# Two-layer graph attention on one core: a new order of the opening loads and projections, two-head folding of a weight, the last sums on TensorE, squares from the evicted copy, and all additions on GpSimd

## The chip, the cores and the metric

One core of a Trainium2 chip runs the whole program. The metric is device time in microseconds (us) of that core; a kernel's figure is the median of its runs. A profile is one further look at one execution; its span is some 2 us shorter than the time of that run.

In this kernel tiles lie in one memory, SBUF, and TensorE writes its products to another, PSUM, in banks; an "eviction" is an instruction of another engine that copies a product out of PSUM. In profile lines PE is TensorE, PEld its weight loads, DVE VectorE, ACT ScalarE and POOL GpSimd. A line of a chain (the work that ended last, followed back) has start and duration in us, engine, tile and line of the kernel; a line of a timeline has the operation and shape too, and in brackets how long the engine sat idle before it and who released it. `x16` merges 16 entries; one product in fp32 shows as two entries. A line of a stretch has its length, then busy time and entries of PE, PEld, DVE, ACT and POOL, the granted clock, and two figures for the DMA.

"Period" is the stretch in which the kernel does one step of its software pipeline; there are 65 of them, and the steady ones are the "middle".

## The reference, cut to what matters

There are 64 graphs of 256 tokens with 512 features. Each passes through two layers of attention over its adjacency.

```python
h = relu(layernorm(x))
# layer 0, 8 heads of 64
m = h @ map_w.T + map_b
n = m / max(norm(m per head), 1e-8);  cos = n @ n.T
p = softmax(mask(q(m) @ k(m).T / 8)) * keep
adj = (cos > 0.1) * p
Ax = adj @ (h @ gcn_map_w.T + gcn_map_b)
out = relu(Ax @ gcn_W.T / (adj.sum(-1) + 1))
x = x + out
# layer 1, 4 heads of 64
x = x + softmax(mask(q1 @ k1.T / 8)) @ v1 @ Wo + bo,  from relu(layernorm(x))
```

`gcn_W` is folded into `gcn_map_w` once at the start, into a weight `wc`, and its bias into `bc`.

## The kernel before

A period works on three graphs: `g` in layer 0, `b` (the one before) in layer 1, and `nx` and `n2` (the next ones) in their projections. TensorE's products go to PSUM through a ring of eight banks. Every call of `bank` takes the next one; it is free when whoever reads it has done so.

```python
def mapped(g):                       # m of a graph, features first
    for n in range(NKC // 2):
        p = features_first(w.wm, g.hT, (2 * n, 2 * n + 1), ...)
        sq = sb2.tile([P, 2, S], F32, tag="sq", ...)
        for k in range(2):
            m = 2 * n + k
            nc.scalar.activation(sq[:, k, :], p[:, k, :], AF.Square, bias=w.bm[:, m:m + 1])
            nc.vector.tensor_scalar_add(g.mT[:, m, :], p[:, k, :], w.bm[:, m:m + 1])

def far_off(g, c, co, eng):          # keeps e where cos > 0.1, and prepares the sums
    g.q[c] = far(co, g.e[c], ...)    # VectorE: a = (co > 0.1) * e, two instructions
    eng.tensor_add(g.e[c], g.e[c], g.q[c])
    g.d[c] = halves(eng, g.e[c], ...)

def period(i):
    ...
    if g:
        spread(g)                                             # p_b
        g.e = [exps(products(g.kT, g.qT, c, ...), ...) for c in range(NKC)]
    if nx:
        mapped(nx)                                            # p_m
    for c in range(NKC):
        if g: co[c] = products(g.nT, g.nT, c, ...)            # co
        if b and c == 1: sc = [products(b.k1T, b.q1T, k, ...) for k in range(NIC)]
        if g and c < 2: far_off(g, c, co[c], nc.gpsimd)
    ...                              # e1 of b, far_off 2 (GpSimd) and 3 (VectorE), d1 of b (VectorE)
    ...                              # messages, queries of nx
    if b:
        values1(b); sums1(b); divided(b)                      # av, zb, then z, rz, oT
    if g:
        values(g, 0); values(g, 1); sums(g)                   # av, sm
    if nx: p_n = norms(nx)
    if b: result(b, 0)                                        # p_o, needs oT
    ...
```

In the opening the weights are loaded and folded first, with temporary tiles; when their pool closes, the tiles of the loop take over its memory. Graphs 0 and 1 are then made ready together.

Of the kernel before, what the change touches and what calls it, by code (L numbers as in the profile page):

```python
# [28 lines left out]
class Weights:  # L29


    def __init__(self, nc, const, tmp, psum, a):
        P, D, DH = 128, a["x"].shape[2], 64
        H0, NKC = D // DH, D // P
        self.ident = const.tile([P, P], F32, name="ident")
        make_identity(nc, self.ident)
        self.ident_b = const.tile([P, P], BF16, name="ident_b")
        nc.vector.tensor_copy(self.ident_b, self.ident)
        self.ones = const.tile([P, DH], F32, name="ones")
        nc.vector.memset(self.ones, 1.0)  # L40
        self.blk = const.tile([P, P], F32, name="blk")
        nc.vector.memset(self.blk, 0.0)
        for j in range(P // DH):
            nc.vector.memset(self.blk[j * DH:(j + 1) * DH, j * DH:(j + 1) * DH], 1.0)



        self.blk32 = const.tile([P, 32], F32, name="blk32")
        nc.vector.memset(self.blk32, 0.0)
        self.sel = const.tile([P, 2, P], F32, name="sel")  # L50
        for j in range(2):
            nc.vector.memset(self.blk32[j * DH:(j + 1) * DH, j * 16:(j + 1) * 16], 1.0)
            for k in range(2):
                r = 32 * k + 16 * j
                nc.vector.tensor_add(self.sel[:, k, j * DH:(j + 1) * DH], self.ident[:, r:r + 1].to_broadcast([P, DH]),
                                     self.ident[:, r + DH:r + DH + 1].to_broadcast([P, DH]))

        def load_w(ap, name):
            t = const.tile([P, ap.shape[0] // P, ap.shape[1]], F32, name=name)
            nc.gpsimd.dma_start(out=t, in_=ap.rearrange("(c p) f -> p c f", p=P))  # L60
            return t

        def load_b(ap, name):
            t = const.tile([P, D // P], F32, name=name)
            nc.gpsimd.dma_start(out=t, in_=ap.rearrange("(c p) -> p c", p=P))
            return t

        self.wm, self.bm = load_w(a["map_wT"], "wm"), load_b(a["map_b"], "bm")
        self.wc = const.tile([P, NKC, D], F32, name="wc")
        self.bc = const.tile([P, D], F32, name="bc")  # L70

        gt = const.tile([DH, DH], F32, name="gt")
        nc.gpsimd.dma_start(out=gt, in_=a["gcn_WT"])
        gb = const.tile([DH, H0], F32, name="gb")
        nc.gpsimd.dma_start(out=gb, in_=a["gcn_map_b"].rearrange("(h j) -> j h", j=DH))
        gbb = tmp.tile([DH, H0, P], F32, name="gbb")
        nc.vector.tensor_copy(gbb, gb[:, :, None].to_broadcast([DH, H0, P]))
        p_bc = psum.tile([P, D], F32, tag="w", name="p_bc")
        for h in range(H0):
            nc.tensor.matmul(p_bc[:, h * DH:(h + 1) * DH], gbb[:, h, :], gt, start=True, stop=True)  # L80
        nc.vector.tensor_copy(self.bc, p_bc)
        gw = tmp.tile([DH, H0, D], F32, name="gw")
        nc.gpsimd.dma_start(out=gw, in_=a["gcn_map_w"].rearrange("(h j) f -> j h f", j=DH))
        for c in range(NKC):
            p_wc = psum.tile([P, D], F32, tag="w", name=f"p_wc{c}")
            for h in range(H0):
                nc.tensor.matmul(p_wc[:, h * DH:(h + 1) * DH], gw[:, h, c * P:(c + 1) * P], gt,
                                 start=True, stop=True)
            nc.vector.tensor_copy(self.wc[:, c, :], p_wc)
        self.wq, self.bq = load_w(a["q_wT"], "wq"), load_b(a["q_b"], "bq")  # L90
        self.wk, self.bk = load_w(a["k_wT"], "wk"), load_b(a["k_b"], "bk")
        self.wq1, self.wk1 = load_w(a["Wq"], "wq1"), load_w(a["Wk"], "wk1")
        self.wv1, self.wo1 = load_w(a["Wv"], "wv1"), load_w(a["Wo"], "wo1")
        self.bo_b = const.tile([P, D], F32, name="bo_b")
        bo = a["bo"]
        nc.gpsimd.dma_start(out=self.bo_b, in_=bass.AP(tensor=bo.tensor, offset=bo.offset, ap=[[0, P], [1, D]]))
# [3 lines left out]
def fast_path(ctx, tc, a, w, chk, out):  # L100
# [30 lines left out]
    def load(i):  # L131
        g = Graph()
        g.i, g.q, g.d = i, {}, {}
# [67 lines left out]
    def mapped(g):  # L201
        g.mT = sb1.tile([P, NKC, S], F32, tag="mT", name=f"mT{g.i}")
        g.sq = []
        for n in range(NKC // 2):
            p = features_first(w.wm, g.hT, (2 * n, 2 * n + 1), f"p_m{g.i}_{n}")
            sq = sb2.tile([P, 2, S], F32, tag="sq", name=f"sq{g.i}_{n}")
            for k in range(2):
                m = 2 * n + k
                nc.scalar.activation(sq[:, k, :], p[:, k, :], AF.Square, bias=w.bm[:, m:m + 1])  # L209
                nc.vector.tensor_scalar_add(g.mT[:, m, :], p[:, k, :], w.bm[:, m:m + 1])  # L210
            g.sq.append(sq)
# [74 lines left out]
    def halves(eng, e, name):  # L286
        d = sb2.tile([P, 2, S], F32, tag="d", name=f"d{name}", bufs=6)
        eng.tensor_add(d, e[:, :, :S], e[:, :, S:])  # L288
# [9 lines left out]
    def far_off(g, c, co, eng):  # L298

        g.q[c] = far(co, g.e[c], f"{g.i}_{c}")  # L300
        eng.tensor_add(g.e[c], g.e[c], g.q[c])  # L301
        g.d[c] = halves(eng, g.e[c], f"0_{g.i}_{c}")
# [7 lines left out]
    def sums(g):  # L310
        sm = bank(f"sm{g.i}")
        for n in range(2):
            for k in range(4):
                nc.tensor.matmul(sm[32 * k:32 * (k + 1), n, :], w.ones[:, :32], g.d[2 * n + k // 2][:, k % 2, :],
                                 start=True, stop=True)
# [33 lines left out]
    def sums1(b):  # L349
        zb = bank(f"zb{b.i}")  # L350
        for c in range(NIC):
            for s in range(2):
                nc.tensor.matmul(zb[s * DH:(s + 1) * DH, c, :], w.ones, b.d1[c][:, s, :], start=True, stop=True)  # L353
# [3 lines left out]
    def divided(b):  # L357
        rz = sb1.tile([P, NIC, S], F32, tag="rz", name=f"rz{b.i}")
# [3 lines left out]
        nc.scalar.activation(b.z, rz, AF.Copy, accum_out=chk[:, b.i, 3:4])  # L362
# [7 lines left out]
    def period(i):  # L370
# [10 lines left out]
        for c in range(NKC):  # L381
# [4 lines left out]
            if g and c < 2:  # L386
                far_off(g, c, co[c], nc.gpsimd)
        if b:
            b.e1 = [exps(sc[k], b.mask1, f"1_{b.i}_{k}") for k in range(NIC)]
        if g:  # L390
            far_off(g, 2, co[2], nc.gpsimd)
            far_off(g, 3, co[3], nc.vector)
        if b:
            b.d1 = [halves(nc.vector, b.e1[k], f"1_{b.i}_{k}") for k in range(NIC)]
# [20 lines left out]
        if nx:  # L415
            p_n = norms(nx)
        if b:
# [45 lines left out]
    with tc.manual_schedule():  # L463
        graphs = {n: load(n) for n in range(min(3, B))}
        for n in range(min(2, B)):
# [5 lines left out]
            graphs[n].hT = turned(graphs[n], f"0_{n}")  # L471
        g = graphs[0]
        mapped(g)
        p_n = norms(g)
# [3 lines left out]
        messages(g, 0)  # L478
        messages(g, 1)
        for n in range(2):  # L480
            queries(g, n)
            keys(g, n)
        for i in range(B + 1):
# [205 lines left out]
def two_layer_kernel(  # L689
# [25 lines left out]
    with tc.tile_pool(name="wtmp", bufs=1) as tmp, \  # L715
            tc.tile_pool(name="wps", bufs=2, space=bass.MemoryType.PSUM) as psum:
        w = Weights(nc, const, tmp, psum, a)
# [48 lines left out]
```

## Time and profile before

| | before |
|---|---|
| time, median of 3 runs | 4140.31 us (4139.12 to 4140.85) |
| span of the profile | 4136.5 us |
| start of period 0 (p_b, the spread of the norms) | 71.13 us |
| one period in the middle | 63.30 us |
| TensorE busy | 4076.0 us |

The lines that bound the kernel are in the prediction. First the chain in one period (start, us, what), then VectorE's timeline, then four entries of the last co products on TensorE, taken with a window of 0.16 us:

```profile
2101.53 1.93 PE co L267 x16
2103.45 1.73 PE sc L267 x16
2105.18 1.98 PE co L267 x15
2107.15 7.06 PE p_s L218 x16
```

```profile
2102.07 0.48 DVE L210 TENSOR_SCALAR mT<-p_m,bm 128x256 f32<-128x256 f32 x1 [1.70 <-ACT sq L209]
2103.10 0.48 DVE L210 TENSOR_SCALAR mT<-p_m,bm 128x256 f32<-128x256 f32 x1 [0.54 <-ACT sq L209]
2103.50 2.47 DVE L282 SCALAR_TENSOR_TENSOR a<-co,e 128x512 f32<-128x512 f32 x4
```

### The profile page before, as it was taken

What the parts mean: (1) busy time and instruction counts of PE and PEld (TensorE: products, weight loads), DVE (VectorE), ACT (ScalarE), POOL (GpSimd) and SP (SyncE); (2) the same over time, 40 slices, a digit from 0 to 9 for tenths busy, and PEclk for the clock granted to TensorE, in tenths of its full rate; (3) what the DMA queues carried; (4) which work ended last, traced back from release to release, by engine and by line L of the source; (5) the groups of instructions that cost most, each with busy time, mean ns of one, the idle gap of its engine ahead of it and who ended that gap; (6) DMA issues with size and microseconds to landing.
All of it is one profiled execution on the core that took longest, in us unless ns stands there. A gap on an engine that the chain in (4) does not pass through costs nothing.

```text
span 4136.5 us, 56746 instructions
## 1 busy us (share of the span) xinstructions
PE 4076.0 (99%) x23633; PEld 3099.0 (75%) x23633; DVE 2649.1 (64%) x3415; ACT 1480.4 (36%) x3138; POOL 1332.9 (32%) x788
## 2 busy tenths in 40 slices
PE   8999999999999999999999999999999999999997
PEld 6777777777777777777777777777777777777774
DVE  3576576676665766766766657667667566576674
ACT  2433433333333333333333333333333433333332
POOL 2233233232332432333323324323333233233232
PEclk9999999999999999999999999999999999999998
DMA  2000000000000000000000000000000000000000
GB/s 87 12 17 17 23 12 22 22 12 23 22 12 23 13 21 22 12 23 22 12 23 20 14 23 12 22 23 12 22 22 12 23 17 17 23 12 22 22 6 16
DMA packets 54389, 81.57 MB, mean 20 GB/s; under 512 B 19744, under 2 KB 19760, under 8 KB 54128
## 3 DMA queue, kind: packets, MB, share of 16 engines
q1 hardware_dynamic: 52224, 71.32, 5.2%
q0 software_dynamic: 1904, 6.58, 0.5%
q8 instruction: 188, 3.08, 0.3%
q14 instruction: 73, 0.60, 0.0%
HBM read 44.33 MB, written 33.55 MB: 19 GB/s over the span
## 4 chain that ended last, share of the span: by engine, by line
PE 91%; DVE 6%; ACT 2%; issue 0%; DMA 0%; POOL 0%; ACTq 0%; POOLq 0%; DVEq 0%
PE p_k L177 16%; PE p_q L177 16%; PE p_m L177 11%; PE p_s L218 11%; PE sc L267 8%; PE co L267 6%; PE p_o L367 6%; PE p_v L452 5%; DVE rz L359 5%; PE av L295 3%; PE p_t L167 3%; PE p_b L238 2%; PE zb L353 1%; PE p_l L336 1%; ACT z L362 1%; ACT z L355 1%
## 5 line engine op out<-in xcount | busy, mean ns | idle before, releaser
L301 POOL TENSOR_TENSOR e<-e,a 128x1024 f32<-128x1024 f32 x192 | 576.5, 3003 | 1719.9 <-DVE a L282 1719.9
L275 DVE TENSOR_TENSOR e<-e,mask 128x1024 f32<-128x1024 f32 x384 | 593.1, 1599 | 142.6 <-ACT e L274 142.6
L242 DVE TENSOR_TENSOR nT<-mT,p_b 128x512 f32<-128x512 f32 x128 | 82.2, 683 | 727.1 <-PE p_b L238 727.1
L177 PE MATMUL p_m<-hT,wm 128*128 128x256 f32 x2048 | 459.8, 383 | 0.0
L218 PE MATMUL p_s<-wc,hT 128*128 128x512 f32 x1024 | 456.6, 599 | 0.0
L177 PE MATMUL p_k<-mT,wk 128*128 128x256 f32 x2048 | 452.8, 379 | 0.0
L177 PE MATMUL p_q<-mT,wq 128*128 128x256 f32 x2048 | 452.6, 379 | 0.0
L177 PEld LDWEIGHTS p_q<-mT,wq 128*128 128x128 f32 x2048 | 389.1, 190 | 80.2 <-issue 30.6
L177 PEld LDWEIGHTS p_m<-hT,wm 128*128 128x128 f32 x2048 | 384.5, 190 | 70.7 <-ACT e L274 20.9
L250 ACT ACTIVATE qT<-p_q,bq 128x256 f32<-128x256 f32 x256 | 107.5, 471 | 889.9 <-PE p_q L177 889.9
L177 PEld LDWEIGHTS p_k<-mT,wk 128*128 128x128 f32 x2048 | 384.2, 190 | 49.6
L274 ACT ACTIVATE e<-sc 128x512 f32<-128x512 f32 x768 | 389.7, 618 | 80.3 <-PE sc L267 79.6
L340 POOL TENSOR_TENSOR xs<-xs,o 128x512 f32<-128x512 f32 x128 | 159.9, 1271 | 783.9 <-DVE o L338 783.9
L218 PEld LDWEIGHTS p_s<-wc,hT 128*128 128x128 f32 x1024 | 189.3, 190 | 235.6 <-issue 235.3
L288 DVE TENSOR_TENSOR d<-e 128x512 f32<-128x512 f32 x192 | 344.3, 1844 | 2.2
L288 POOL TENSOR_TENSOR d<-e 128x512 f32<-128x512 f32 x192 | 318.5, 1659 | 15.1
L282 DVE SCALAR_TENSOR_TENSOR a<-co,e 128x512 f32<-128x512 f32 x512 | 316.2, 677 | 0.0
L267 PE MATMUL co<-nT 64*128 64x256 f32 x2048 | 266.3, 387 | 1.2 <-DVE a L282 1.2
L367 PE MATMUL p_o<-wo,oT 128*128 128x512 f32 x512 | 248.9, 609 | 15.6 <-ACT z L362 10.5
L359 DVE RECIPROCAL rz<-z 128x512 f32<-128x512 f32 x64 | 214.6, 3354 | 71.5 <-ACT z L355 71.5
L210 DVE TENSOR_SCALAR mT<-p_m,bm 128x256 f32<-128x256 f32 x256 | 123.2, 481 | 186.5 <-ACT sq L209 186.5
L439 POOL TENSOR_TENSOR xs<-xs,bo_b 128x512 f32<-128x512 f32 x128 | 171.0, 1356 | 221.5 <-DVE xn L158 217.8
(113 smaller groups left out, 5920.6 us busy)
## 6 DMA issues: line engine op xcount, KB each, us to landing
xs<-in_x_dram SPq DMA_DIRECT2D x64, 512.0 KB, 3.8
out_dram<-xs SPq DMA_DIRECT2D x64, 512.0 KB, 2.8
ad<-in_adj_dram SPq DMA_DIRECT2D x64, 64.0 KB, 3.6
wm<-in_L_gnn_map_w_dram POOLq DMA_DIRECT2D x1, 1024.0 KB, 6.2
gw<-in_L_gnn_gcn_map_w_dram POOLq DMA_DIRECT2D x1, 1024.0 KB, 9.0
wq<-in_L_gnn_q_w_dram POOLq DMA_DIRECT2D x1, 1024.0 KB, 10.9
wk<-in_L_gnn_k_w_dram POOLq DMA_DIRECT2D x1, 1024.0 KB, 12.5
wq<-in_L_gnn_Wq_dram POOLq DMA_DIRECT2D x1, 512.0 KB, 12.4
```

The source lines that it names most:

```text
L177: nc.tensor.matmul(p[:, n, :], wt[:, c, m * P:(m + 1) * P], src[:, c, :], start=(c == 0), stop=(c == nk - 1))
L218: nc.tensor.matmul(p, g.hT[:, c, t * P:(t + 1) * P], w.wc[:, c, :], start=(c == 0), stop=(c == NKC - 1))
L267: nc.tensor.matmul(ps[s][:, j, :], rows[h, c, j * P:(j + 1) * P], cols[h, c, :], start=True, stop=True)
L274: nc.scalar.activation(e[:, s, :], p.rearrange("p j q -> p (j q)"), AF.Exp, scale=SCALE)
L275: nc.vector.tensor_mul(e, e, mask[:, None, :].to_broadcast([P, 2, NT * S]))
L282: nc.vector.scalar_tensor_tensor(q[:, s, :], p.rearrange("p j q -> p (j q)"), THRESHOLD, e[:, s, :], op0=ALU.is_gt, op1=ALU.mult)
L288: eng.tensor_add(d, e[:, :, :S], e[:, :, S:])
L301: eng.tensor_add(g.e[c], g.e[c], g.q[c])
L359: nc.vector.reciprocal(rz, b.z)
L367: nc.tensor.matmul(p, b.oT[:, c, t * P:(t + 1) * P], w.wo1[:, c, :], start=(c == 0), stop=(c == NIC - 1))
L439: nc.gpsimd.tensor_add(g.xs[:, t, :], g.xs[:, t, :], w.bo_b)
L452: nc.tensor.matmul(p[:, t, :], hT[:, c, t * P:(t + 1) * P], w.wv1[:, c, :], start=(c == 0), stop=(c == NKC - 1))
```

## The change

Its intent is to shorten the opening (x requested at once, the fold behind the first projection and in half as many products, graph 1 made ready behind graph 0's projections), to shorten the end (no additions of the last graph ahead of its sums), and to relieve VectorE.

```diff
-        for h in range(H0):                     # fold: 40 products, one head each
-            nc.tensor.matmul(p_wc[:, h*DH:(h+1)*DH], gw[:, h, c*P:(c+1)*P], gt, ...)
+        for k in range(NKC):                    # fold: 20, two heads each, gt block diagonal
+            nc.tensor.matmul(p[:, k*P:(k+1)*P], gws[k//2][:, k%2, c*P:(c+1)*P], self.gt, ...)
...
         for n in range(NKC // 2):
             p = features_first(w.wm, g.hT, (2 * n, 2 * n + 1), ...)
+            for m in (2 * n, 2 * n + 1):
+                nc.vector.tensor_scalar_add(g.mT[:, m, :], p[:, m - 2 * n, :], w.bm[:, m:m + 1])
             sq = sb2.tile([P, 2, S], F32, tag="sq", ...)
-            for k in range(2):
-                m = 2 * n + k
-                nc.scalar.activation(sq[:, k, :], p[:, k, :], AF.Square, bias=w.bm[:, m:m + 1])
-                nc.vector.tensor_scalar_add(g.mT[:, m, :], p[:, k, :], w.bm[:, m:m + 1])
+            nc.scalar.activation(sq, g.mT[:, 2 * n:2 * n + 2, :], AF.Square)
...
-            far_off(g, 3, co[3], nc.vector)     # and d1 of b on VectorE
+            far_off(g, 3, co[3])                # all additions on GpSimd, d1 ahead of far_off 2
...
     def sums(g):
+                if g.last:                      # no additions: four parts into one sum
+                    parts = [t[:, s, j*S:(j+1)*S] for t in (g.e[c], g.q[c]) for j in range(NT)]
+                else:
+                    parts = [g.d[c][:, s, :]]
+                for m, part in enumerate(parts):
+                    nc.tensor.matmul(sm[32*k:32*(k+1), n, :], w.ones[:, :32], part, ...)
...
     def divided(b):
-        nc.scalar.activation(b.z, rz, AF.Copy, accum_out=chk[:, b.i, 3:4])   # now ahead of result(b, 0)
...
-        graphs = {n: load(n) for n in range(min(3, B))}     # after the fold
-        # graphs 0 and 1 ready, mapped(0), norms, messages(0), queries and keys(0)
+        graphs = {0: load(0)}                               # first of all
+        # other loads; graph 0 ready, mapped(0), fold, norms, queries and keys(0),
+        # graph 1 ready, messages(0)
```

More of the change, by code (lines that the diff above doesn't have):

```diff
@@ L29, with __init__ @@
 class Weights:
-    def __init__(self, nc, const, tmp, psum, a):
+    def __init__(self, nc, const, a):
         P, D, DH = 128, a["x"].shape[2], 64
-        H0, NKC = D // DH, D // P
+        self.nc, self.const, self.a = nc, const, a
         self.ident = const.tile([P, P], F32, name="ident")
         make_identity(nc, self.ident)
+        self.wm, self.bm = self.load_w("map_wT", "wm"), self.load_b("map_b", "bm")
+        self.gt = const.tile([P, P], F32, name="gt")
+        nc.vector.memset(self.gt, 0.0)
+        for j in range(2):
+            nc.scalar.dma_start(out=self.gt[j * DH:(j + 1) * DH, j * DH:(j + 1) * DH], in_=a["gcn_WT"])
+        self.gb = const.tile([P, D // P], F32, name="gb")
+        nc.scalar.dma_start(out=self.gb, in_=a["gcn_map_b"].rearrange("(c p) -> p c", p=P))
         self.ident_b = const.tile([P, P], BF16, name="ident_b")
@@ L42, in __init__ @@
         nc.vector.memset(self.blk, 0.0)
-        for j in range(P // DH):
+        for j in range(2):
             nc.vector.memset(self.blk[j * DH:(j + 1) * DH, j * DH:(j + 1) * DH], 1.0)
@@ L56, in __init__ @@
                                      self.ident[:, r + DH:r + DH + 1].to_broadcast([P, DH]))
-        def load_w(ap, name):
-            t = const.tile([P, ap.shape[0] // P, ap.shape[1]], F32, name=name)
-            nc.gpsimd.dma_start(out=t, in_=ap.rearrange("(c p) f -> p c f", p=P))
-            return t
-        def load_b(ap, name):
-            t = const.tile([P, D // P], F32, name=name)
-            nc.gpsimd.dma_start(out=t, in_=ap.rearrange("(c p) -> p c", p=P))
-            return t
-        self.wm, self.bm = load_w(a["map_wT"], "wm"), load_b(a["map_b"], "bm")
@@ L69, in __init__ @@
-        self.wc = const.tile([P, NKC, D], F32, name="wc")
-        self.bc = const.tile([P, D], F32, name="bc")
-        gt = const.tile([DH, DH], F32, name="gt")
-        nc.gpsimd.dma_start(out=gt, in_=a["gcn_WT"])
-        gb = const.tile([DH, H0], F32, name="gb")
-        nc.gpsimd.dma_start(out=gb, in_=a["gcn_map_b"].rearrange("(h j) -> j h", j=DH))
-        gbb = tmp.tile([DH, H0, P], F32, name="gbb")
-        nc.vector.tensor_copy(gbb, gb[:, :, None].to_broadcast([DH, H0, P]))
-        p_bc = psum.tile([P, D], F32, tag="w", name="p_bc")
@@ L79, in __init__, with load_w @@
-        for h in range(H0):
-            nc.tensor.matmul(p_bc[:, h * DH:(h + 1) * DH], gbb[:, h, :], gt, start=True, stop=True)
-        nc.vector.tensor_copy(self.bc, p_bc)
-        gw = tmp.tile([DH, H0, D], F32, name="gw")
-        nc.gpsimd.dma_start(out=gw, in_=a["gcn_map_w"].rearrange("(h j) f -> j h f", j=DH))
+        self.wc = const.tile([P, D // P, D], F32, name="wc")
+        self.bc = const.tile([P, D], F32, name="bc")
+    def load_w(self, key, name):
+        ap = self.a[key]
+        t = self.const.tile([128, ap.shape[0] // 128, ap.shape[1]], F32, name=name)
+        self.nc.gpsimd.dma_start(out=t, in_=ap.rearrange("(c p) f -> p c f", p=128))
+        return t
@@ new lines, in load_b, with load_rest @@
+    def load_b(self, key, name):
+        ap = self.a[key]
+        t = self.const.tile([128, ap.shape[0] // 128], F32, name=name)
+        self.nc.scalar.dma_start(out=t, in_=ap.rearrange("(c p) -> p c", p=128))
+        return t
+    def load_rest(self):
+        self.wq, self.bq = self.load_w("q_wT", "wq"), self.load_b("q_b", "bq")
+        self.wk, self.bk = self.load_w("k_wT", "wk"), self.load_b("k_b", "bk")
+        self.wv1 = self.load_w("Wv", "wv1")
+        self.wq1, self.wk1 = self.load_w("Wq", "wq1"), self.load_w("Wk", "wk1")
+        self.wo1 = self.load_w("Wo", "wo1")
+        bo = self.a["bo"]
+        self.bo_b = self.const.tile([128, bo.shape[0]], F32, name="bo_b")
+        self.nc.gpsimd.dma_start(out=self.bo_b, in_=bass.AP(tensor=bo.tensor, offset=bo.offset,
+                                                            ap=[[0, 128], [1, bo.shape[0]]]))
@@ new lines, in load_folded, with fold @@
+    def load_folded(self, gws):
+        gw = self.a["gcn_map_w"].rearrange("(c p) f -> p c f", p=128)
+        for k, t in enumerate(gws):
+            self.nc.gpsimd.dma_start(out=t, in_=gw[:, 2 * k:2 * k + 2, :])
+    def fold(self, gws, gbb, bank):
+        nc, P = self.nc, 128
+        NKC = self.wc.shape[1]
+        nc.vector.tensor_copy(gbb, self.gb[:, :, None].to_broadcast([P, NKC, P]))
+        p = bank("p_bc", [P, NKC * P])
+        for k in range(NKC):
+            nc.tensor.matmul(p[:, k * P:(k + 1) * P], gbb[:, k, :], self.gt, start=True, stop=True)
+        nc.vector.tensor_copy(self.bc, p)
@@ L84, in __init__ @@
         for c in range(NKC):
-            p_wc = psum.tile([P, D], F32, tag="w", name=f"p_wc{c}")
-            for h in range(H0):
-                nc.tensor.matmul(p_wc[:, h * DH:(h + 1) * DH], gw[:, h, c * P:(c + 1) * P], gt,
+            p = bank(f"p_wc{c}", [P, NKC * P])
+            for k in range(NKC):
+                nc.tensor.matmul(p[:, k * P:(k + 1) * P], gws[k // 2][:, k % 2, c * P:(c + 1) * P], self.gt,
                                  start=True, stop=True)
-            nc.vector.tensor_copy(self.wc[:, c, :], p_wc)
@@ L90, in __init__ @@
-        self.wq, self.bq = load_w(a["q_wT"], "wq"), load_b(a["q_b"], "bq")
-        self.wk, self.bk = load_w(a["k_wT"], "wk"), load_b(a["k_b"], "bk")
-        self.wq1, self.wk1 = load_w(a["Wq"], "wq1"), load_w(a["Wk"], "wk1")
-        self.wv1, self.wo1 = load_w(a["Wv"], "wv1"), load_w(a["Wo"], "wo1")
-        self.bo_b = const.tile([P, D], F32, name="bo_b")
-        bo = a["bo"]
-        nc.gpsimd.dma_start(out=self.bo_b, in_=bass.AP(tensor=bo.tensor, offset=bo.offset, ap=[[0, P], [1, D]]))
+            nc.vector.tensor_copy(self.wc[:, c, :], p)
@@ L132, in load @@
         g = Graph()
-        g.i, g.q, g.d = i, {}, {}
+        g.i, g.last, g.q, g.d = i, i == B - 1, {}, {}
         g.xs = io.tile([P, NT, D], F32, tag="xs", name=f"xs{i}")
@@ L284, in far, with halves @@
         return q
-    def halves(eng, e, name):
+    def halves(e, name):
         d = sb2.tile([P, 2, S], F32, tag="d", name=f"d{name}", bufs=6)
-        eng.tensor_add(d, e[:, :, :S], e[:, :, S:])
+        nc.gpsimd.tensor_add(d, e[:, :, :S], e[:, :, S:])
         return d
@@ L296, in weighed, with far_off @@
                                  q[:, s, j * S:(j + 1) * S], start=(j == 0), stop=(j == NT - 1))
-    def far_off(g, c, co, eng):
+    def far_off(g, c, co):
         g.q[c] = far(co, g.e[c], f"{g.i}_{c}")
-        eng.tensor_add(g.e[c], g.e[c], g.q[c])
-        g.d[c] = halves(eng, g.e[c], f"0_{g.i}_{c}")
+        if not g.last:
+            nc.gpsimd.tensor_add(g.e[c], g.e[c], g.q[c])
+            g.d[c] = halves(g.e[c], f"0_{g.i}_{c}")
     def values(g, n):
@@ L313, in sums @@
             for k in range(4):
-                nc.tensor.matmul(sm[32 * k:32 * (k + 1), n, :], w.ones[:, :32], g.d[2 * n + k // 2][:, k % 2, :],
-                                 start=True, stop=True)
+                c, s = 2 * n + k // 2, k % 2
+                if g.last:
+                    parts = [t[:, s, j * S:(j + 1) * S] for t in (g.e[c], g.q[c]) for j in range(NT)]
+                else:
+                    parts = [g.d[c][:, s, :]]
+                for m, part in enumerate(parts):
+                    nc.tensor.matmul(sm[32 * k:32 * (k + 1), n, :], w.ones[:, :32], part,
+                                     start=(m == 0), stop=(m == len(parts) - 1))
         nc.scalar.activation(g.sms, sm, AF.Copy, accum_out=chk[:, g.i, 0:1])
@@ L352, in sums1 @@
             for s in range(2):
-                nc.tensor.matmul(zb[s * DH:(s + 1) * DH, c, :], w.ones, b.d1[c][:, s, :], start=True, stop=True)
+                parts = [b.e1[c][:, s, j * S:(j + 1) * S] for j in range(NT)] if b.last else [b.d1[c][:, s, :]]
+                for m, part in enumerate(parts):
+                    nc.tensor.matmul(zb[s * DH:(s + 1) * DH, c, :], w.ones, part,
+                                     start=(m == 0), stop=(m == len(parts) - 1))
         b.z = sb1.tile([P, NIC, S], F32, tag="z", name=f"z{b.i}")
@@ L357, in divided @@
     def divided(b):
-        rz = sb1.tile([P, NIC, S], F32, tag="rz", name=f"rz{b.i}")
+        rz = b.rz = sb1.tile([P, NIC, S], F32, tag="rz", name=f"rz{b.i}")
         nc.vector.reciprocal(rz, b.z)
@@ L386, in period @@
             if g and c < 2:
-                far_off(g, c, co[c], nc.gpsimd)
+                far_off(g, c, co[c])
         if b:
             b.e1 = [exps(sc[k], b.mask1, f"1_{b.i}_{k}") for k in range(NIC)]
+            if not b.last:
+                b.d1 = [halves(b.e1[k], f"1_{b.i}_{k}") for k in range(NIC)]
         if g:
-            far_off(g, 2, co[2], nc.gpsimd)
-            far_off(g, 3, co[3], nc.vector)
-        if b:
-            b.d1 = [halves(nc.vector, b.e1[k], f"1_{b.i}_{k}") for k in range(NIC)]
+            far_off(g, 2, co[2])
+            far_off(g, 3, co[3])
         if nx:
@@ L416, in period @@
             p_n = norms(nx)
+        if b:
+            nc.scalar.activation(b.z, b.rz, AF.Copy, accum_out=chk[:, b.i, 3:4])
         if b:
@@ L463, in fast_path, with first @@
     with tc.manual_schedule():
-        graphs = {n: load(n) for n in range(min(3, B))}
-        for n in range(min(2, B)):
+        graphs = {0: load(0)}
+        gws = [sb2.tile([P, 2, D], F32, tag="e", name=f"gw{k}", bufs=6) for k in range(2)]
+        w.load_folded(gws)
+        graphs.update({n: load(n) for n in range(1, min(3, B))})
+        w.load_rest()
+        def first(n):
             edges(graphs[n])
@@ L471, in fast_path @@
             graphs[n].hT = turned(graphs[n], f"0_{n}")
+        first(0)
         g = graphs[0]
         mapped(g)
+        w.fold(gws, sb2.tile([P, NKC, P], F32, tag="o", name="gbb"), bank)
         p_n = norms(g)
@@ L477, in fast_path @@
         nc.vector.reciprocal(g.rn, g.rn)
-        messages(g, 0)
-        messages(g, 1)
         for n in range(2):
@@ L482, in fast_path @@
             keys(g, n)
+        if B > 1:
+            first(1)
+        messages(g, 0)
+        messages(g, 1)
         for i in range(B + 1):
@@ L714, in two_layer_kernel @@
     const = ctx.enter_context(tc.tile_pool(name="const", bufs=1))
-    with tc.tile_pool(name="wtmp", bufs=1) as tmp, \
-            tc.tile_pool(name="wps", bufs=2, space=bass.MemoryType.PSUM) as psum:
-        w = Weights(nc, const, tmp, psum, a)
+    w = Weights(nc, const, a)
     B = x.shape[0]
```

## The prediction

> **What bounds the kernel now.** I read the page's busy line and chain first, then a table of stretches, then the timelines of one period, then the two ends.
>
> ```profile
> PE 4076.0 (99%) x23633; PEld 3099.0 (75%) x23633; DVE 2649.1 (64%) x3415; ACT 1480.4 (36%) x3138; POOL 1332.9 (32%) x788
> PE 91%; DVE 6%; ACT 2%; issue 0%; DMA 0%; POOL 0%; ACTq 0%; POOLq 0%; DVEq 0%
> ```
>
> TensorE is busy for 4076.0 of 4136.5 us and is 91% of the chain that ended last. The other 60.5 us are all that better overlap can win. Where are they? Stretches (PE, PEld, DVE, ACT, POOL busy, then clock):
>
> ```profile
> 0.00:20.00 20.00, 10.05 (x46) 9.86 (x47) 3.72 (x16) 1.28 (x1) 11.16 (x20) 1.00 0.85 239
> 20.00:40.00 20.00, 12.08 (x59) 11.31 (x59) 8.25 (x19) 3.83 (x9) 1.71 (x4) 1.00 0.63 209
> 264.00:328.00 64.00, 63.83 (x373) 48.67 (x372) 41.75 (x54) 23.07 (x49) 20.72 (x12) 1.00 0.05 18
> 4060.00:4080.00 20.00, 11.47 (x52) 6.14 (x54) 17.59 (x16) 1.65 (x4) 13.91 (x6) 0.57 0.00 1
> ```
>
> In the middle PE idles 0.17 us in 64. A period is 63.30 us (the first GpSimd addition starts at 2104.92 and again at 2168.22). The idle is in the opening (17.9 us before 40) and at the end. So only the two ends can gain; the middle can only lose. The chain through the opening:
>
> ```profile
> 4.60 8.98 DMA gw<-in_L_gnn_gcn_map_w_dram
> 13.62 13.93 PE p_wc L87 x64
> 27.57 3.94 DMA xs<-in_x_dram
> 40.43 7.63 PE p_m L177 x32
> 71.13 1.06 PE p_b L238 x8
> ```
>
> The first x is not even requested until 27.57, just after the folding of the weights ends: the tiles of the loop reuse the memory of the temporary weight pool, so x waits for the fold. Period 0 begins at 71.13.
>
> **What the Trainium skill says.** (1) "TensorE: Matmul & The Clock Gate", Part 1 (The HAM clock gate): the array runs at half clock until one activity window (3413 ns) was busy, and falls back when idle. The trace agrees: eight transposes took 1.97 us at 34.93, later 0.88. The stretch table's 1.00 for the opening isn't what those matmuls show. (2) Same page, Part 3 (The mechanism): matmuls start and end in strict program order; only weight loads are pulled ahead. [...]No serial case is in this trace; the alternating case is (16 entries of the sums in 1.0 us). (3) "SBUF — State Buffer", Who interferes with whom: a VectorE instruction with two SBUF inputs excludes a GpSimd one that reads SBUF. The trace agrees: the mask product takes 1.16 us alone (4 in 4.63) and 2.33 beside GpSimd (2 in 4.67). (4) "GPSIMD Engine Reference", 3.1: an addition costs about 2x VectorE's. Here 1.26 against 0.64 us undisturbed.
>
> **The change, part by part.**
>
> Opening. The temporary pool goes, so x0 is requested at about 0.9 and lands near 5. But the masks' transposes precede the turned x on TensorE, and need a GpSimd cast (0.6 us) that now stands behind ten weight requests on GpSimd. GpSimd's requests show a limit:
>
> ```profile
> 7.77 0.75 POOL L65 DMA_DIRECT2D bk<-in_L_gnn_k_b_dram  x1 [0.23 <-DMA wm<-in_L_gnn_map_w_dram]
> 13.86 0.70 POOL L60 DMA_DIRECT2D wo<-in_L_gnn_Wo_dram  x1 [2.76 <-DMA gw<-in_L_gnn_gcn_map_w_dram]
> GB/s 0 53 360 268 197 197 291 331 391 300 354 360 186 0 171 290 294 358 74 0 0 0 0 0 0 0 0 0 0 0 0 0 0 8 0 0 0 0 0 0
> ```
>
> The 9th request waits for the 1st, the 13th for the 5th: eight are outstanding (the third line is the first 80 us in 2 us slices). In the new order the 9th (wo1) waits for wm and the 10th (bo_b) for the first half of the fold's weights. Ahead of that half go x0 to x2 with adj, 3 x 0.59 MB, wm 1.05, and its own 0.52: 3.3 MB, at some 330 GB/s (estimate from the slices) 10 us, from 2.5: about 13. Then the request 0.6 and the cast 0.6: TensorE's first work at 14.4. From there, all durations from the opening's chain and timeline:
> - cold transposes and eviction, 0.6+2.0+0.6: the m projection starts at 17.6 (before: 40.43).
> - it takes 7.0 warm; cold for its first 5 us (no full busy window came before) costs 2.6: 27.2.
> - the fold is now right behind it and needs the bias spread on VectorE, behind two mT evictions: 2 x 0.48 + 0.69 + latencies 0.25 = 1.9 us idle: 29.1.
> - fold: 20 products instead of 40, over 128 columns; 20 x 2 passes x 0.108 us (rt's pace for this shape) = 4.3, against 13.9 + 3.7 cold before. The 1.9 us gap may let the clock fall; I add 1.0: 34.4.
> - norms 0.6, queries and keys 4 x 3.45 = 13.8 (weights landed by 21: 5.9 MB), graph 1's mask and transposes 1.1, messages 7.06: period 0 at 57.0.
> Gain 71.1 - 57.0 = 14.1 us. The fold's own saving is part of this, not additional.
>
> Middle. Per period GpSimd takes over one e addition (2.21 on VectorE) and three halvings (5.42). Its additions run from 2104.92 to 2119.0 now; the sums that need the last one begin on TensorE at 2127.25:
>
> ```profile
> 2104.92 2.35 POOL L301 TENSOR_TENSOR e<-e,a 128x1024 f32<-128x1024 f32 x1 [26.59 <-DVE a L282]
> 2117.48 1.60 POOL L288 TENSOR_TENSOR d<-e 128x512 f32<-128x512 f32 x1
> 2127.25 1.07 PE L314 MATMUL sm<-d,ones 128*32 128x256 f32 x16
> ```
>
> New queue: 4 x (2.35+1.26) + 2 x 1.26 = 17.0, plus 2 x 1.16 for the two mask products that still exclude it: 19.3. It starts 1.1 earlier (VectorE no longer alternates mT with ScalarE's squares): 2103.8 + 19.3 = 2123.1, 4 us before it is needed. At today's mean pace (3.00 and 1.66, plus nothing) it is 4 x 4.66 + 3.3 = 22.0: 2125.8, still in time. The squares (one of 512 columns instead of two of 256) and the moved check copy are ScalarE work; ScalarE is at 36%. The 0.17 us before p_o follows VectorE's oT, which still waits for the 3.35 us reciprocal, so it stays. Middle: 0.
>
> End. For the last graph VectorE's e addition (2.21) and halvings (4.39 in the chain) go, 2 mask products are undisturbed (2 x 1.16 saved): the last far-off product ends at 4067.3 and zb starts near 4067.5 instead of 4076.32, an 8.8 us lead. But sums take 32 products instead of 8, and the loop runs the four parts of one column tile in succession. In strict order a product holds its tile 2 x 0.216 us and only the last of four overlaps the next tile: 8 x 3 x 0.432 + 0.4 = 10.8 us instead of 1.0. Values end near 4072.0, so sums at 4082.9 against 4083.5: 0.6 gained of 8.8. The last b has 8 zb products instead of 4, pairs in series: +1.0. End: about 0. If tiles run independently, 32 x 0.432/4 = 3.5 us and the end gains 7. I give strict order 75 in 100: expected gain 1.5.
>
> Sum: 4140.3 - 14.1 - 0 - 1.5 = 4124.7 us, 0.4% less.
>
> **The rivals.** (a) GpSimd becomes the bound of the middle: its busy share would rise from 32% to about 44%, and sums would wait. Each us late is 63 us (+1.5%). Against it: the margin of 1.5 to 4 us. If port exclusion stretched all its additions to 3.33+2.13, the queue would be 26 us and 2.6 us late: 4290. (b) No blocking of the cast in the opening, if the weights land earlier: TensorE starts at 9 to 10 and the opening gains 19; with independent tiles too, 4114. (c) The loads contend so that wm and the first half of gw land only at 16 or 17: gain 11; with strict order and a colder end, 4131. (d) A faster middle, because VectorE is relieved: VectorE was not what TensorE waited for (0.17 us in 64), so at most 0.17 x 63 = 11 us.
>
> **Range and chances.** Opening 10 to 20 and end -2 to 7 give 4115 to 4132. 2% is 83 us, more than all idle time of TensorE, so faster has 0.01; slower needs rival (a), 0.03; within 2%, 0.96.
>
> **What would show it.** Opening: first x requested below 1.5 us, a GpSimd request waiting for wm and one for gw ahead of the cast, spread at 57 (51 to 61). Middle: PE busy 63.8 of 64, sums' wait absent, GpSimd's last halving 1 us or more before sums. End: sums' starts 0.43 us apart on one tile and some 11 us in all; 3.5 would make the end's step wrong. A period above 63.4 us would make the middle wrong.

## More of the kernel before

```profile
2105.66 0.85 PE L267 MATMUL co<-nT 64*128 64x256 f32 x4
```

Shown are the chain in one period (start, us, what) and four entries of the last co products on TensorE, taken with a window of 0.16 us. The reader is to see that VectorE's second eviction of a pair waits 0.54 us for ScalarE's square, that the four far-off products follow directly behind, and that the same shape of product takes 1.73 us for 16 entries in the middle line of the chain and 1.98 us in the third.

## The result

The changed kernel took 4104.18 us (median of 4 runs, 4103.53 to 4105.31) against 4140.44 us for the kernel before in the same rounds: 36.3 us less, where 15.6 were predicted. The ratio is 0.9913 (95% interval 0.9896 to 0.993). A ratio is the mean time of one kernel's fast runs over that of the other's of the same rounds, so it isn't quite the ratio of the medians that are quoted.

Where the time went can be read from three marks in each kernel's chain: the start of period 0, the start of the last full period (both are TensorE's p_b), and the start of the last instruction.

| part of the span, us | before | after | gained | predicted |
|---|---|---|---|---|
| opening, to period 0 | 71.13 | 56.06 | 15.1 | 14.1 |
| middle, period 0 to period 63 | 3979.97 | 3964.48 | 15.5 | 0 |
| end, from period 63 | 79.34 | 75.24 | 4.1 | 1.5 (0 or 7) |

The three parts add up to 34.7 us; the two profiled spans differ by 34.5, and the rest of the 36.3 lies between single executions. The opening came as worked out. The middle gained 0.24 us in each period, which the prediction had ruled out. The page of the changed kernel, its busy line, then the stretch of 64 us that was shown of the kernel before:

```profile
PE 4050.7 (99%) x23649; PEld 3072.0 (75%) x23649; DVE 2233.5 (54%) x3160; ACT 1453.2 (35%) x3010; POOL 1559.9 (38%) x1030
```

```profile
264.00:328.00 64.00, 63.83 (x374) 48.60 (x373) 35.79 (x52) 22.65 (x47) 25.52 (x18) 1.00 0.06 18
```

The stretch is as busy as before: 63.83 of 64. Yet the period went from 63.30 to 63.06 us. So the gain isn't in what the profile counts as idle: TensorE's recorded busy time fell by 25.3 us (4076.0 to 4050.7), the middle's 15.5 among them. The same three places of the middle as above, in the changed kernel:

```profile
2141.62 1.93 PE co L280 x16
2143.54 1.73 PE sc L280 x16
2145.27 1.73 PE co L280 x16
2147.00 7.06 PE p_s L231 x16
```

```profile
2141.65 0.88 DVE L221 TENSOR_SCALAR mT<-p_m,bm 128x256 f32<-128x256 f32 x2 [1.83 <-PE p_m L191]
2142.71 2.48 DVE L295 SCALAR_TENSOR_TENSOR a<-co,e 128x512 f32<-128x512 f32 x4 [0.18 <-PE co L280]
```

```profile
2145.75 0.60 PE L280 MATMUL co<-nT 64*128 64x256 f32 x4
```

The third group of products now takes 1.73 us instead of 1.98, and that is the whole gain of a period. The far-off products start 1.16 us after the first co product (2142.71 against 2141.55 in TensorE's timeline); before it was 2.05 us (2103.50 against 2101.45). The four entries take 0.60 us instead of 0.85.

The opening in the chain of the changed kernel:

```profile
12.32 0.57 POOL bo_b L87
12.89 0.63 POOL adb L199
13.56 0.61 PE p_a L208 x4
...
16.56 9.05 PE p_m L191 x32
...
26.51 0.34 DVE gbb L100
26.86 0.04 issue
26.90 1.16 PE p_bc L103 x8
28.06 3.57 PE p_wc L108 x32
...
56.06 1.06 PE p_b L251 x8
```

TensorE's first work waits for the cast, and the cast stands behind GpSimd's request for bo_b, as foreseen. The end, from the chain:

```profile
4040.78 8.10 PE sm L334 x64
```

The sums took 8.10 us: neither the 10.8 of strict order nor the 3.5 of independent tiles.

### The profile page after: what moved, and what is told of

Same layout as the page of the kernel before. It is cut to its first block, busy times and chain, and to the rows that moved or that the text cites. A ratio compares the mean times of both kernels' runs of the same rounds, so it can differ in the third digit from the quotient of the medians.

```text
span 4102.0 us, 56638 instructions
## 1 busy us (share of the span) xinstructions
PE 4050.7 (99%) x23649; PEld 3072.0 (75%) x23649; DVE 2233.5 (54%) x3160; ACT 1453.2 (35%) x3010; POOL 1559.9 (38%) x1030
## 4 chain that ended last, share of the span: by engine, by line
PE 91%; DVE 6%; ACT 1%; issue 0%; DMA 0%; POOL 0%; ACTq 0%; POOLq 0%; DVEq 0%
PE p_q L191 16%; PE p_k L191 16%; PE p_m L191 11%; PE p_s L231 11%; PE sc L280 8%; PE p_o L389 6%; PE co L280 6%; PE p_v L476 5%; DVE rz L382 5%; PE av L308 3%; PE p_t L181 3%; PE p_b L251 2%; PE zb L375 1%; PE p_l L356 1%; DVE oT L384 1%; ACT z L378 1%
## 5 line engine op out<-in xcount | busy, mean ns | idle before, releaser
L315 POOL TENSOR_TENSOR e<-e,a 128x1024 f32<-128x1024 f32 x252 | 654.7, 2598 | 1649.9 <-DVE a L295 1649.9
L288 DVE TENSOR_TENSOR e<-e,mask 128x1024 f32<-128x1024 f32 x384 | 563.8, 1523 | 164.6 <-ACT e L287 164.6
L301 POOL TENSOR_TENSOR d<-e 128x512 f32<-128x512 f32 x378 | 528.7, 1413 | 42.9 <-DVE e L288 23.1
L389 PE MATMUL p_o<-wo,oT 128*128 128x512 f32 x512 | 248.3, 608 | 15.4 <-DVE oT L384 15.3
L280 PE MATMUL co<-nT 64*128 64x256 f32 x2048 | 251.4, 384 | 1.2 <-DVE a L295 1.2
L476 PEld LDWEIGHTS p_v<-wv,hT 128*128 128x128 f32 x1024 | 194.5, 190 | 54.1 <-ACT hT L182 15.5
L476 PE MATMUL p_v<-wv,hT 128*128 128x256 f32 x1024 | 231.6, 379 | 0.4 <-ACT hT L182 0.4
```

Of the source, the lines that this page charges most:

```text
L280: nc.tensor.matmul(ps[s][:, j, :], rows[h, c, j * P:(j + 1) * P], cols[h, c, :], start=True, stop=True)
L288: nc.vector.tensor_mul(e, e, mask[:, None, :].to_broadcast([P, 2, NT * S]))
L301: nc.gpsimd.tensor_add(d, e[:, :, :S], e[:, :, S:])
L315: nc.gpsimd.tensor_add(g.e[c], g.e[c], g.q[c])
L389: nc.tensor.matmul(p, b.oT[:, c, t * P:(t + 1) * P], w.wo1[:, c, :], start=(c == 0), stop=(c == NIC - 1))
L476: nc.tensor.matmul(p[:, t, :], hT[:, c, t * P:(t + 1) * P], w.wv1[:, c, :], start=(c == 0), stop=(c == NKC - 1))
```

## The experiments

All kernels gave correct results. The marks above are used for each; they are from one profile each, and the opening and the end of nearly equal code differ by up to 2.5 us between profiles (openings of the kernel before and of its single edits of the middle: 70.28 to 72.74 us), the middle by less than 0.4.

**Theories.** A: the fourth far-off product of VectorE frees a PSUM bank too late for the fourth co product, because the evictions ahead of it alternate with ScalarE's squares; TensorE's wait is hidden in overlapping records. B: the additions that moved to GpSimd relieved VectorE or ended the exclusion between the two engines.

### Single edits on the kernel before, and one undone

`sq_alone` takes the new `mapped` alone.

> The kernel before with one edit: the squares read the evicted copy, so the two evictions of a projected pair follow each other on VectorE. Theory A (late bank): the middle's gain of 15.5 us comes from here, because the fourth far-off product of VectorE then frees its PSUM bank before TensorE wants it: 4125 us (15 less), period 63.06 us instead of 63.30, and the third group of co products 0.25 us shorter. Theory B (additions moved to GpSimd relieve VectorE): 4140 us, period 63.30.

Measured: 4126.16 us against 4139.25, ratio 0.9966 (0.995 to 0.9983). The middle took 3964.69 us, a period 63.06. All of the middle's gain is there.

`sq_order` keeps ScalarE's squares from PSUM and only turns the order:

```diff
-            for k in range(2):
-                nc.scalar.activation(sq[:, k, :], p[:, k, :], AF.Square, bias=...)
-                nc.vector.tensor_scalar_add(g.mT[:, 2 * n + k, :], p[:, k, :], ...)
+            for m in (2 * n, 2 * n + 1):
+                nc.vector.tensor_scalar_add(g.mT[:, m, :], p[:, m - 2 * n, :], ...)
+            for m in (2 * n, 2 * n + 1):
+                nc.scalar.activation(sq[:, m - 2 * n, :], p[:, m - 2 * n, :], AF.Square, bias=...)
```

> The kernel before, squares still read from PSUM by ScalarE in two instructions of 256 columns with bias, but both evictions on VectorE come ahead of them in the program. Theory A says that only the alternation of the two engines on one bank cost time, not where the squares read: 4125 us, as with the evicted copy. If the source of the squares matters (ScalarE's reads of PSUM, or the bank held longer), it stays near 4140 us. Theory B: 4140 us.

Measured: 4126.02 us, ratio 0.9969 (0.9952 to 0.9985), middle 3964.58 us. Where the squares read from doesn't matter here; what costs time is that they alternate with the evictions.

`pool_adds` moves the additions alone:

```diff
-            far_off(g, 3, co[3], nc.vector)
-        if b:
-            b.d1 = [halves(nc.vector, b.e1[k], ...) for k in range(NIC)]
+            far_off(g, 3, co[3], nc.gpsimd)      # and d1 on GpSimd, ahead of far_off 2
```

> The kernel before with all additions on GpSimd in the order of the changed kernel, nothing else. Theory A: the middle keeps its period of 63.30 us, 4140 us to 4142 us (the very end a little different, as the last graph's additions are now all on the slower engine: up to 3 us more). Theory B: 4125 us and a period of 63.06 us.

Measured: 4137.29 us against 4139.25, ratio 0.9995 (0.9978 to 1.0012), a period 63.30, middle 3979.98 us. Theory B falls. My side remark on the end was wrong in sign: with d1 ahead in GpSimd's queue, zb ran from 4071.11 us (4076.32 before) and the values ran beside the remaining additions, so the sums ended at 4080.6 in place of 4083.5, in a period that started 0.8 us earlier.

`undo_sq` is the changed kernel with the old squares.

> The changed kernel with the old squares (from PSUM, alternating with the evictions). Theory A: the middle loses what it gained: 4119 to 4120 us and a period of 63.30 us. Theory B: stays at 4104 us. If the two edits only work together, both this and the single edits lie between.

Measured: 4121.4 us, ratio to before 0.9957 (0.994 to 0.9973), a period 63.30, middle 3979.85 us. It lost 15.4 us of middle, the whole gain (the time is 1.4 us above the expected range; its opening took 57.36 us instead of 56.06).

`check_late` moves ScalarE's check copy alone behind the norms.

> The kernel before with ScalarE's check copy moved behind the norms, nothing else. The page put the 0.17 us ahead of p_o down to that copy. My step said it follows VectorE's oT: then no change, 4140 us, period 63.30. If it was the copy, 0.17 x 63 = 11 us less.

Measured: 4139.16 us against 4139.4, ratio 0.9998 (0.9981 to 1.0015), middle 3979.71 us. The page's releaser for p_o (the check copy) was the one that ended last by 0.04 us, not the one that mattered.

### Doses of delay

If theory A holds, VectorE may be late by a little at no cost, and then each further tenth costs. In the changed kernel I let VectorE evict the same 256 columns again, straight ahead of the far-off products.

```diff
             nc.scalar.activation(sq, g.mT[:, 2 * n:2 * n + 2, :], AF.Square)
+            if n == 1 and g.i > 0:
+                for _ in range(K):               # one_extra: K = 1, three_extra: K = 3
+                    nc.vector.tensor_scalar_add(g.mT[:, 3, :], p[:, 1, :], w.bm[:, 3:4])
```

> The changed kernel with the fourth eviction of each projection done once more on VectorE (same values; 0.40 us per period, straight ahead of the far-off products). In the changed kernel the fourth far-off product ends some 0.73 us before TensorE needs its bank. Theory A (a late bank costs, an early one doesn't): 0.40 us fits in that slack, 4104 us, period 63.06. If VectorE's work there counted in proportion, 0.40 x 63 = 25 us more: 4129.

> The same with the eviction done three times more (1.2 us per period). Theory A: the bank is now 0.45 us late, so the period grows by about 0.45 to 0.6 us: 4132 to 4142 us, and the third group of co products is stretched. If the bank had nothing to do with it, 4104 us; in proportion 76 us more: 4180.

Measured: 4122.25 us (ratio 0.9958, 0.9942 to 0.9975) and 4166.56 us (ratio 1.0063, 1.0046 to 1.0079). Both are misses. The profile of `one_extra` shows why; VectorE's timeline:

```profile
2153.03 0.48 DVE L226 TENSOR_SCALAR mT<-p_m,bm 128x256 f32<-128x256 f32 x1 [0.70 <-ACT sq L223]
2153.43 2.47 DVE L298 SCALAR_TENSOR_TENSOR a<-co,e 128x512 f32<-128x512 f32 x4
```

The extra eviction overwrites what ScalarE's square reads, so it waits 0.70 us for it. The dose was far more than 0.40. `one_clean` and `two_clean` put one and two extra evictions ahead of the square in the program, where nothing holds them.

> The changed kernel with the fourth eviction done twice ahead of the square in the program, so that, unlike in one_extra, it doesn't wait for ScalarE: VectorE's far-off products start 0.40 us later per period and nothing else. In the changed kernel the fourth product ends 0.73 us before TensorE needs the bank. Theory A: no loss, 4104 to 4106 us, period 63.06. If VectorE's work there counts in proportion, 4129 us.

> The same done three times ahead of the square: 0.80 us later, about as late as in the kernel before (0.89). Theory A: the bank is just late: period 63.15 to 63.30, 4110 to 4120 us. In proportion: 4154 us. If the slack is larger than worked out: 4104 us.

Measured: 4103.61 us (ratio to before 0.9913, the changed kernel's own) and 4114.75 us (ratio 0.994). With the two misses and both kernels this gives one row of six doses. The first column is the start of the first far-off product less that of the first co product, each from the timelines of one period:

| | far-off behind co, us | period, us |
|---|---|---|
| after | 1.16 | 63.06 |
| one_clean | 1.42 | 63.05 |
| two_clean | 1.94 | 63.20 |
| before | 2.05 | 63.30 |
| one_extra | 2.09 | 63.34 |
| three_extra | 3.13 | 64.04 |

`one_clean` shifted the start by 0.26 us only, as VectorE had waited 0.18 us for co anyway. It cost nothing, where a cost in proportion would have moved it; between 1.94 and 2.09 a delay of 0.15 us costs 0.14 us. So there is a threshold somewhere between 1.42 and 1.94 us, and the kernel before stood beyond it. This is what a late bank does. Where exactly the threshold lies, no run shows. The first co products, the far-off products and the last co products in one period of `one_clean`, then of `two_clean`:

```profile
2142.17 2.00 PE L282 MATMUL co<-nT 64*128 64x256 f32 x16
2143.59 2.48 DVE L297 SCALAR_TENSOR_TENSOR a<-co,e 128x512 f32<-128x512 f32 x4
2145.72 1.89 PE L282 MATMUL co<-nT 64*128 64x256 f32 x16
```

```profile
2146.89 2.00 PE L283 MATMUL co<-nT 64*128 64x256 f32 x16
2148.83 2.47 DVE L298 SCALAR_TENSOR_TENSOR a<-co,e 128x512 f32<-128x512 f32 x4
2150.45 2.04 PE L283 MATMUL co<-nT 64*128 64x256 f32 x16
```

The single records show what a late bank costs. In `two_clean`, the kernel before and `one_extra` the product that waits starts 0.04, 0.14 and 0.18 us later than in the changed kernel, each time 0.05 us after VectorE's fourth far-off product ends. Its weight load is then recorded together with it, and not 0.21 us ahead as in the changed kernel, and its second entry follows the first after 0.32 us instead of 0.22. Wait and these 0.10 us make 0.14, 0.24 and 0.28, which is what the periods lost in the table. That the load's place causes the 0.10 us is argued, not tried.

`three_extra` doesn't extend this row. There the second layer-1 score product (sc) waits for the last extra eviction as well, three co products start 0.05 us after a far-off product each, and the last one starts 0.17 us before the fourth far-off product ends, so it can't have waited for that.

### The end, the opening, and the last gap

`sums_turns` lets the four parts be the outer loop and the tiles the inner.

```diff
-                for m, part in enumerate(parts):          # inside: for k in range(4)
-                    nc.tensor.matmul(sm[32 * k:32 * (k + 1), n, :], ...)
+            for m in range(2 * NT if g.last else 1):
+                for k in range(4):
+                    nc.tensor.matmul(sm[32 * k:32 * (k + 1), n, :], ...)
```

> The changed kernel with the last graph's sums in turns over the column tiles (the part is the outer loop, the tile the inner), and the same for the last zb. If tiles run side by side only when neighbours in program order use different tiles, the 64 entries of the sums take 3.5 to 4 us instead of 8.10 and zb 1.8 to 2.0 instead of 2.11: 4099 to 4100 us. If the order doesn't matter, 4104 us.

Measured: 4101.4 us (ratio 0.9906, 0.9889 to 0.9922; the changed kernel had 4104.18 in other rounds), 1.4 us above the expected range. The same line of the chain:

```profile
4041.75 3.59 PE sm L335 x64
```

3.59 us, as four tiles side by side allow. The end was 72.6 us instead of 75.2; the sums alone saved 4.5, and the rest was lost elsewhere in the end, in the same profile: b's values ahead of them took 2.60 us instead of 1.88, at a granted clock of 0.72 in that stretch, where the changed kernel's profile has 1.00. The last zb, expected at 1.8 to 2.0 us, took 2.77 at 0.65 (2.11 at 0.88 in the changed kernel), so what turns do there isn't shown. The end's figure carries about that much chance.

`cast_first` puts the cast of graph 0's mask ahead of the ninth weight request.

```diff
         self.wq1, self.wk1 = self.load_w("Wq", "wq1"), self.load_w("Wk", "wk1")
+        between()                                 # edges(graphs[0])
         self.wo1 = self.load_w("Wo", "wo1")
```

> The changed kernel with the cast of graph 0's mask on GpSimd ahead of the ninth weight request, which waits for wm to land. If the blocked GpSimd queue holds the opening, TensorE's first transposes start near 8 us instead of 13.56 and the m projection near 10.5 to 11 (when wm has landed) instead of 16.56, period 0 up to 5.5 us earlier: 4098.5 to 4100 us. If the opening is held by the transfers anyway, 4104 us.

Measured: 4099.87 us (ratio 0.9904, 0.9887 to 0.992). TensorE's first work began at 8.97 us instead of 13.56, the m projection at 11.95 instead of 16.56, period 0 at 51.05 instead of 56.06.

`zb_first` turns `values1(b); sums1(b)` round.

> The changed kernel with zb's sums ahead of the values of the same graph on TensorE, so that the reciprocal and oT end 1.8 us earlier. If oT is what p_o waits for, the 0.17 us of idle time per period goes: period 62.89, 4093 to 4094 us. If something else holds p_o, 4104 us.

Measured: 4090.57 us (ratio 0.9881, 0.9865 to 0.9898), a period 62.84. A stretch of 64 us:

```profile
1000.00:1064.00 64.00, 64.00 (x375) 48.78 (x374) 36.09 (x51) 22.64 (x47) 24.57 (x16) 1.00 0.05 18
```

TensorE is busy for all of it. The gain was 0.21 to 0.22 us per period where the idle row had 0.17: again a wait cost more than its row.

`combined` joins these with two more moves of the opening.

> The changed kernel with sums in turns, the cast first, zb first, the bias spread of the fold before the m projection, and graph 1's statistics ahead of the queries. Sum of the parts: 4.4 + 5 + 10.5 + 1.3 + 1.7 = 23 us less: 4081 us, 4078 to 4088.

Measured: 4087.09 us, 6 above the sum of the parts and at the upper end of the stated range. Its chain in the opening has the cause:

```profile
2.51 13.14 DMA gb<-in_L_gnn_gcn_map_b_dram
15.65 0.02 issue
15.68 0.04 DVE gbb L510
```

I had moved the bias spread (gbb) ahead on VectorE, but its 2 KB land at 15.65 us, and VectorE's cast of the identity, which the first transposes need, came behind it: the first transposes started at 16.29. `combined_b` leaves the bias spread where the changed kernel has it.

> The combined kernel without moving the bias spread ahead (it waited for the bias to land at 15.65 us and held VectorE, and with it the mask's cast of the identity and the transposes). Sum of the parts as measured: 4087 less the 6.9 us by which the opening was later than in cast_first with its 1.7 us wait taken out: 4080 us, 4077 to 4083.

Measured: 4079.5 us (4078.62 to 4080.02), ratio to before 0.9855 (0.9839 to 0.9872): 24.7 us below the changed kernel's median of other rounds (their ratios to before are 0.9855 and 0.9913). Period 0 starts at 49.43, a period is 62.84. It beats both kernels.

One more kernel, the kernel before with memory of its own for the temporary weights, couldn't be built: the loop's tiles didn't fit beside them. How much of the opening's 15 us is due to the early request alone is therefore open.

## Why the prediction was wrong

**The opening was right.** 57.0 us was worked out for the start of period 0; it was 56.06. Term by term: TensorE's first work 13.56 us (14.4), m projection 16.56 (17.6) to 25.61 (27.2), idle ahead of the fold 1.29 (1.9), fold 4.73 us (4.3 and 1.0 for a colder clock). A wait that wasn't foreseen, 1.67 us for graph 1's turned x, whose ScalarE square root was queued behind the evictions of the keys, took back most of what these terms had saved (the fold ended 2.8 us earlier than worked out, period 0 began 0.9 earlier), so that the sum came out this close is in part luck. `combined_b`, which takes graph 1's statistics ahead of the queries, has no such wait; its period 0 starts 1.6 us before `cast_first`'s. The trap of the ten weight requests was real, as `cast_first` shows: 5.0 us lay in it.

**The middle was wrong, and it carries the miss.** The step that failed is this one: "In the middle PE idles 0.17 us in 64. [...] So only the two ends can gain; the middle can only lose", and with it rival (d), which bounded any gain of VectorE's relief by that idle time, at 11 us. The runs showed 15.5 us gained there, and the prediction's sign of a wrong middle looked only for a longer period. The idle row was read as a bound on waits, and it isn't one: an entry of these products is recorded with 0.38 us while the next starts 0.22 us later, so records overlap, and a wait of up to 0.16 us disappears between them. In the kernel before, VectorE's fourth far-off product ended at 2105.97 us; in the single records of the trace the product on one tile half had started at 2105.88 and its partner, which needs that bank, at 2106.03. From there the two halves ran out of step to the end of the group; the late product's second entry came 0.32 us after its first instead of 0.22, and 0.14 us of wait became 0.24 us of time. The sign stood in the trace before the change: 16 entries of one shape in 1.73 us in one line of the chain, and 15 recorded ones in 1.98 in the next line.

**A fact was on the table and used for one thing only.** The prediction noted that VectorE's far-off products start 1.1 us earlier because mT no longer alternates with the squares (0.89 measured, against the co products) and used that for GpSimd's queue. It didn't ask which bank those products free, nor when TensorE wants it. `sq_order`, `undo_sq` and the doses show that this was the whole gain of the middle.

**GpSimd did not become the bound.** Worked out: last halving 2123.1 against sums at 2127.25, 4 us of slack. Measured in the changed kernel, from GpSimd's and TensorE's timelines:

```profile
2098.81 1.27 POOL L301 TENSOR_TENSOR d<-e 128x512 f32<-128x512 f32 x1
2104.03 1.07 PE L334 MATMUL sm<-d,ones 128*32 128x256 f32 x16
```

The last halving ends at 2100.08, 3.95 us ahead of the sums. The means of its additions fell to 2.60 and 1.41 us (3.00 and 1.66 before): in one period the last two e additions take 2.36 us each, where the last one before took 3.33 beside VectorE's own additions. Rival (a) was rightly given little.

**The gap ahead of p_o stayed, as said.** `check_late` changed nothing and the changed kernel still has 0.17 us there; `zb_first`, which lets oT end 1.7 us earlier, took it away.

**At the end a term was mis-sized.** The lead came: the sums began 20.2 us after their period's p_b (4040.78 against 4020.54) instead of 31.4 (4082.51 against 4051.10), 11.2 us sooner (10.5 was worked out). The sums were put at 10.8 us if in strict order, or at 3.5; they took 8.10. The single records show why: the first entry of the next tile started at 4041.60, together with the third product of the tile before, not with its fourth. Two tiles ran side by side throughout, so the strict order to which the prediction gave 75 in 100 didn't hold, nor did independent tiles. Of the 11.2 us the longer sums gave back 7.1, and the end gained 4.1, between the two cases; what came after the sums changed little in all. The extra on the last zb was right (2.11 us instead of 1.24; 1.0 was worked out).

**A slip in a sum.** The low end of the stated range, 4115 us, doesn't follow from its own extremes: openings of 20 and an end of 7 give 4113. The measured time lies below both.

## What to carry to other kernels

A busy share near 100% doesn't say that an engine runs at its pace: compare the duration of equal groups of instructions in the chain, and follow every PSUM bank from the read that frees it to the product that takes it next. Don't let two engines take turns on one PSUM tile in the program: put all of one engine's reads ahead, above all the one whose queue carries the later work (here 0.24 us of each period). Before moving an instruction to the front of an in-order queue, look up when its input lands, and on TensorE let consecutive products address different column tiles.

## What the Trainium skill lacked or had wrong

- "TensorE: Matmul & The Clock Gate", Part 3 (The mechanism), says that matmuls start and end in program order. In the changed kernel's sums, taken in the order of kernel.py, the entries of the next column tile started at 4041.60 us, with the third of four products of the tile before and ahead of its fourth (4042.03); 64 entries took 8.10 us where strict order gives 10.8 and turns over the tiles took 3.59.
- No page has what a bank that comes free late costs when two tiles run as a pair: waits of 0.04, 0.14 and 0.18 us on one of them cost 0.14, 0.24 and 0.28 us a period, some 0.10 us more than the wait each time.
- "Perfetto Trace Analysis", Tensor Engine Instruction (MATMUL, LD_WEIGHTS), rightly says that the recorded end of a matmul is an estimate. It doesn't say what follows: entries recorded with 0.38 us start every 0.22 us, so TensorE was 63.83 us busy of 64 both at 63.30 and at 63.06 us a period.
- No page says how many requests a GpSimd queue of such a program keeps under way. Here the ninth waited for the first (0.23 us in the kernel before, 2.89 in the changed one, where it was in front of work that TensorE needed). Whether the chip or the program sets that number, no run shows.
